# Residual adds between blocks, copies of the first unit's fourth slab, and VectorE in written order

## The chip, the cores and the metric

The kernel runs on one core of one Trainium2 chip. The metric is the time of one execution on the device in microseconds (us); lower is better. The core has a matrix engine (TensorE, PE in the profile), three engines for elementwise work (VectorE or DVE, ScalarE or ACT, GpSimd or POOL) and SyncE (SP), whose queue issues nearly all DMA transfers here. Each engine takes its own instructions in a fixed order and waits for the others by semaphores. TensorE writes its results to PSUM, in banks of 128 x 512 float32 values; tiles that are kept longer lie in SBUF.

## The reference

Eight sequences `x[b]` of 512 rows and 256 columns go through nine gated experts (eight with a gate per sequence and expert, and a shared one), and the input is added at the end. All is float32.

```python
g = jnp.einsum('bsd,edf->ebsf', h, Wg)
u = jnp.einsum('bsd,edf->ebsf', h, Wu)
expert_outs = jnp.einsum('ebsf,efd->ebsd', jax.nn.silu(g) * u, Wd)
expert_output = jnp.einsum('be,ebsd->bsd', gating_probs, expert_outs)
shared = jnp.einsum('bsf,fd->bsd', jax.nn.silu(h @ Sg) * (h @ Su), Sd)
return (1.0 - sg) * expert_output + sg * shared
# and then: x = x + that
```

The hidden size F is 1024.

## The kernel before

**Tiling.** The eight sequences form two halves (`h` = 0, 1) of four. Within a half, each expert's hidden columns are cut into two groups (`g`) of four slabs of 128 columns. A half, an expert and a group make a *unit*: 2 x 9 x 2 = 36 units, one after the other. A unit multiplies four sequences by four slabs. It does so with fewer products than the plain way: sums and differences of the operands are formed, for the four points `CI` = 0, 1, -1, 2 and the six pairs of `PAIRS`, and the results are put together from them.

**A unit on TensorE.** `hub_steps` lists the steps on the four diagonal combinations: `P_step` (L458) starts a bank, `Q_step` (L481) adds to it. From the bank's state after P, ScalarE keeps a copy `P` (L464, slabs 0 to 2), and VectorE forms differences `f` between slabs (L474, L476); for slab 3 they read the bank itself and overwrite the copies. After Q, ScalarE makes `sg` = silu(bank) (L444) or VectorE makes `h` = sg x gate x bank (L449), for the gate half (m = 0) and the up half (m = 1); ScalarE keeps `D`, a copy of the bank (L488, L491). Then come the six pairs. For each pair, `seed` fills a bank from `f` (L498, ScalarE), `R1_step` adds a product of `v` (a difference of inputs) and `u` (one of weights) to it (L503), and at once makes the bank of the other direction, `D` minus this one (L508, VectorE). `R_step` adds the products of `b` and `wb` to both banks (L513); for the second direction VectorE adds `D` (L518). Their `h` go to `h_sums`, which makes `X`, the difference of the pair's two `h` (L529), and notes the sums of `h` that GpSimd adds later (L540, `rows` and `cols`).

**The down product** of a unit (`down`) runs interleaved with the second half of the same unit and the first half of the next one. `pair` makes three steps for each pair: `r` (L595), then `S` or `s` (L579, L595), then the product with `X` on top of `r` (L618). Its results are collected in accumulators in SBUF: `accB`, `accV` and `accb`, by VectorE (L566 to L570). For pairs 0 to 3 `S` is carried on: ScalarE copies `accS` into a PSUM bank (L578), TensorE adds to it, ScalarE copies it back (L587); `b` likewise. Two PSUM banks (`po0`, `po1`) serve all of this in turn. In the last `down` of each half (`closes`) the accumulators are combined (L622).

**The order.** The strings `ORDER`, `FIRST` and `LAST` write out how gate/up steps (G), down steps (D), input turns (T) and the last unit's products (X) alternate: a unit is `HUB` (GGD eight times) and six times `BLOCK` (GGDGGDGGD). The engines in `HAND` (L843: PE and Pool; for the first unit ScalarE too, L846) take their instructions as written. VectorE's and the other engines' instructions are placed by a scheduler. `AHEAD_AT` and `BACK_AT` name the D steps at which `prepare` (the second half's inputs) and `turn_back` do a piece.

**First unit.** Its inputs are turned on TensorE; `v` and `b` are computed by VectorE and GpSimd (`x_difference`, `x_sums`) and stored to DRAM, from where all later units load them (L292, L309). `v` tiles share three buffers, `b` two, `wb` two.

**Ends of the halves.** Results are kept transposed, in 32 x 32 squares. For the first half, `turn_back` (L663) reloads the sequence from DRAM into a tile of `iopool` (two buffers; L659), transposes a result on VectorE (L669), adds it (L670) and issues four stores (L673). These pieces run in the second half's first unit. For the last unit, `end_step` turns what is there so far, stores it to DRAM as rows and loads it back (`endin`, L707), loads the input rows (L150), lets GpSimd add both (L711), and `store_rows` adds the last products (L729) and stores.

Of the kernel before, what the change touches and what calls it, by code (L numbers as in the profile page):

```python
# [16 lines left out]
def kernel(  # L17
# [104 lines left out]
    back = {}  # L122
# [18 lines left out]
    def load_rows(pool, tag, b):  # L141
        rows = []
        for c in range(2):
            if pool is not xpool:
                t = pool.tile([P, 2, D], F32, tag=tag, name=f"xin{b}_{c}")
            elif c == 0:
                both = pool.tile([P, NT, D], F32, tag=tag, name=f"xin{b}")
            if pool is xpool:
                t = both[:, 2 * c : 2 * c + 2]
            nc.sync.dma_start(  # L150
                t, x[b].rearrange("(p t) d -> p t d", t=NT)[:, 2 * c : 2 * c + 2, :]
            )
            rows.append(t)
        return rows


    def squares(a, b, q):

        return a[b].rearrange("s (k q d) -> q s k d", k=2, d=32)[q]
# [122 lines left out]
    def x_difference(u, p):  # L282

        i, j = PAIRS[p]
        v = vpool.tile([P, S], F32, tag="v", name=f"v{u.name}_{p}")
# [169 lines left out]
    def P_step(u, i, m):  # L455
# [6 lines left out]
        if i < 3:  # L462
            t = ppool.tile([P, S], F32, tag="p", name=f"P{i}{m}_{u.name}")
            nc.scalar.copy(t, bank)  # L464
            u.Ps[i, m] = t
        for p, (k, j) in enumerate(PAIRS):
# [33 lines left out]
    def R1_step(u, p, m):  # L500
# [5 lines left out]
        other = new_bank(u, m, f"c{i}{j}")  # L506
        u.bank[i, j, m] = other
        ve.tensor_sub(other, u.Ds[j, m], bank)  # L508
# [142 lines left out]

    BACK = [(0, 1), (0, 0), (2, 1), (2, 0), (1, 1), (1, 0), (3, 1), (3, 0)]

    def load_back(h, i):

        if (h, i) not in back:
            xr = iopool.tile([P, S // 32, 2, 32], F32, tag="io", name=f"xr{h}_{i}")
            for q in range(4):
                nc.sync.dma_start(xr[ts(q, 32)], squares(x, NI * h + i, q))  # L659
            back[h, i] = xr  # L660
        return back[h, i]

    def turn_back(h, i, r):  # L663

        b = NI * h + i
        block = ends.pop((h, i, r))
        xr = load_back(h, i)
        t = zpool.tile([P, S], F32, tag="z", name=f"to{b}_{r}")
        ve.transpose(t, block)  # L669
        ve.tensor_add(xr[:, :, r], t.rearrange("p (c d) -> p c d", d=32), xr[:, :, r])  # L670
        if (i, 1 - r) not in BACK[BACK.index((i, r)):]:
            for q in range(4):
                nc.sync.dma_start(squares(out, b, q), xr[ts(q, 32)])  # L673
            if i in (0, 2):
                load_back(h, i + 1)
# [5 lines left out]
    end_stores = []  # L681

    def end_step(kind, i):

        b = NI * (NH - 1) + i
# [5 lines left out]
        elif kind == "store":  # L691
            to = end_rows[i] = dram.tile([S, D], F32, tag=f"end{i}", name=f"endrows{i}")
            at = to.rearrange("(c r t) d -> r t c d", r=32, t=NT)
            for r in range(2):
                for q in range(4):
                    end_stores.append((
# [3 lines left out]
        elif kind == "x":  # L700
            last_rows[i] = load_rows(xpool, "x", b)
        elif kind == "load":
            at = end_rows[i].rearrange("(p t) d -> p t d", t=NT)
            end_rows[i] = []
            for c in range(2):
                t = sumpool.tile([P, 2, D], F32, tag="sum", name=f"endin{i}_{c}")
                nc.sync.dma_start(t, at[:, 2 * c : 2 * c + 2])  # L707
                end_rows[i].append(t)
        else:
            for xr, t in zip(last_rows[i], end_rows[i]):  # L710
                gp.tensor_tensor(xr, xr, t, ALU.add)  # L711
# [13 lines left out]
    def store_rows(j, c):  # L725
        b = NI * (NH - 1) + j
        xr = last_rows[j][c]
# [12 lines left out]
    def gate_up(u, nxt):  # L740
# [18 lines left out]
        step = 0  # L759
        for kind, i, m in hub_steps(u):  # L760
# [6 lines left out]
            elif kind == "P":  # L767
                P_step(u, i, m)
                if u.n == 0 and m == 1 and i in (1, 3):
                    for p, make in ahead[:2] if i == 1 else ahead[2:]:  # L770
                        make(u, p)
            else:
                R1_step(u, 0, m)
            step += 1
# [5 lines left out]
        if u.n == 0:  # L780
            make_ad(u)
            for p in range(len(PAIRS)):
                d_forms(u, p)
        for p in range(len(PAIRS)):
# [13 lines left out]
            for m in range(2):  # L798
                if not last:
                    R1_step(u, p + 1, m)  # L800
                    if m == 0 and u.n == 0 and p and p + 1 < len(PAIRS):
                        sums(p + 1)
# [3 lines left out]
                for r in range(2):  # L806
                    R_step(u, p, m, r)
                    if m == 1 and r == 1:
# [3 lines left out]
                        if p + 2 < len(PAIRS) and u.n:  # L812
                            sums(p + 2)
# [15 lines left out]
        7: (("turn", 0), ("store", 0)), 16: (("turn", 1), ("store", 1)), 18: (("x", 0),),  # L829
        20: (("turn", 2), ("store", 2), ("x", 1)), 22: (("load", 0), ("x", 2)),  # L830
        24: (("turn", 3), ("store", 3), ("x", 3)), 28: (("add", 0),), 30: (("load", 1),),
        34: (("add", 1),), 37: (("load", 2),), 40: (("add", 2),), 44: (("load", 3),),
        47: (("add", 3),),
# [7 lines left out]
    AHEAD_AT = (8, 11, 14, 17, 20)  # L841
    BACK_AT = (6,10,11,13,15,18,20,23)
    HAND = {mybir.EngineType.PE, mybir.EngineType.Pool}  # L843
    by_hand = ExitStack()
    by_hand.enter_context(
        tc.manual_schedule(engines=HAND | {mybir.EngineType.Activation})  # L846
# [18 lines left out]
    for u in units:  # L865
# [6 lines left out]
        for what in FIRST if u.n == 0 else LAST if nxt is None else ORDER:  # L872
            if what == "G":
                if nG == TAKE:
                    for _ in behind:
                        pass
                    if u.opens:
                        acc = {}
                    behind = down(u, acc) if nxt is not None else iter(())
                if final and nxt is not None and nG in (18, 21, 24, 27):  # L880
                    load_x(u.h + 1, (nG - 18) // 3)
                if final and nxt is not None and nG in (30, 36):
                    load_back(u.h, (nG - 30) // 3)
                if nxt is None:
                    for what_, i in END_STEPS.get(nG, ()):
                        end_step(what_, i)
                    if end_stores:
# [71 lines left out]
```

## Time and profile before

Three runs took 2445.75, 2446.47 and 2447.15 us. One execution was profiled.

| what | value |
|---|---|
| median of the runs | 2446.47 us |
| the profiled execution, its own time | 2446.47 us |
| its span, first to last instruction | 2444.7 us |
| TensorE clock granted, mean | 0.999 |
| wait of a `b` load for landing, median from issue | 3.6 us |
| one `X` (L529), mean | 982 ns |
| one `h` (L449), mean | 743 ns |

The page gives, for each engine, the time in which it was busy and the number of its instructions. A group of instructions is named by its source line, engine and operation, and `out<-in` by the program's tile names with their numbers left out. A float32 matmul of 128 x 512 appears as two passes. A timeline row holds the start from the beginning of the span, the duration, the engine, the line, the operation and, in brackets, how long the engine had been idle before it and what released it. A wait row holds the waiting engine and its line, what it waited for, the total in us, how often, and the longest.

### The profile page before, as it was taken

How to read it: one execution, taken by the hardware profiler on the slowest of the kernel's cores; microseconds unless marked ns; L12 is line 12 of the kernel's file. 1: busy time of each engine (PE TensorE's matmuls, PEld its weight loads, DVE VectorE, ACT ScalarE, POOL GpSimd, SP SyncE). 2: the span in 40 equal slices, each digit the busy share in tenths (PEclk: the TensorE clock that was granted, in tenths of full speed). 3: DMA queues.
4: the chain of work that ended last, by engine and by line, in shares of the span. 5: the costliest groups of instructions: out<-in, count | busy, mean ns of one | idle time of the engine just before them, and what ended most of it. 6: DMA issues, size and time to landing. Idle time of an engine off the chain costs nothing.

```text
span 2444.7 us, 22778 instructions
## 1 busy us (share of the span) xinstructions
PE 2431.5 (99%) x5736; PEld 1085.1 (44%) x5736; DVE 1928.9 (79%) x2870; ACT 1239.4 (51%) x2294; POOL 2080.0 (85%) x2313
## 2 busy tenths in 40 slices
PE   9999999999999999999999999999999999999999
PEld 4444444444444444444444444444444444444446
DVE  7778878777777877787987777777777777777795
ACT  5555554554555555555445555555555555555542
POOL 8988888898988989898878888888888888888872
PEclk9999999999999999999999999999999999999999
DMA  4333343343433333344353233323333333233245
GB/s 158 101 105 111 104 112 112 103 134 102 126 110 97 105 111 97 106 129 125 112 118 120 85 95 91 91 81 99 99 104 103 95 97 92 88 91 92 86 117 149
DMA packets 237841, 260.02 MB, mean 106 GB/s; under 512 B 80656, under 2 KB 173072, under 8 KB 237712
## 3 DMA queue, kind: packets, MB, share of 16 engines
q1 hardware_dynamic: 236880, 258.27, 35.9%
q8 instruction: 48, 0.79, 0.1%
q14 instruction: 81, 0.66, 0.1%
q10 hardware_dynamic: 832, 0.30, 0.0%
HBM read 240.69 MB, written 17.83 MB: 106 GB/s over the span
## 4 chain that ended last, share of the span: by engine, by line
PE 96%; POOL 1%; DVE 1%; DMA 1%; issue 0%; ACT 0%; SPq 0%; ACTq 0%; DVEq 0%; POOLq 0%
PE c L513 30%; PE c L503 15%; PE c L481 10%; PE c L458 10%; PE r L595 7%; PE r L618 7%; PE S L579 5%; PE b L579 5%; PE q L595 5%; PE s L595 2%; PE tail L720 1%; DMA sgt<-ondB_sharedgateprob_dram 0%; POOL wd L429 0%; POOL wb L396 0%; DVE h L449 0%
## 5 line engine op out<-in xcount | busy, mean ns | idle before, releaser
L513 PE MATMUL c<-b,wb 128*128 128x512 f32 x1728 | 848.1, 593 | 2.6 <-DMA b<-xs 1.9
L444 ACT ACTIVATE sg<-c 128x512 f32<-128x512 f32 x576 | 343.8, 597 | 595.0 <-DVE c L518 343.7
L449 DVE SCALAR_TENSOR_TENSOR h<-sg,coef,c 128x512 f32<-128x512 f32 x576 | 427.8, 743 | 235.6 <-PE c L513 128.3
L513 PEld LDWEIGHTS c<-b,wb 128*128 128x128 f32 x1728 | 328.3, 190 | 412.9 <-issue 390.0
L503 PE MATMUL c<-v,u 128*128 128x512 f32 x864 | 441.5, 593 | 1.9 <-ACT c L498 1.4
L540 POOL TENSOR_TENSOR rows<-rows,h 128x512 f32<-128x512 f32 x280 | 369.0, 1318 | 0.0
L508 DVE TENSOR_TENSOR c<-D,c 128x512 f32<-128x512 f32 x432 | 298.7, 692 | 81.1 <-ACT sg L444 61.4
L540 POOL TENSOR_TENSOR cols<-cols,h 128x512 f32<-128x512 f32 x280 | 357.7, 1277 | 0.0
L518 DVE TENSOR_TENSOR c<-c,D 128x512 f32<-128x512 f32 x432 | 298.6, 691 | 22.3 <-PE c L513 22.1
L396 POOL TENSOR_TENSOR wb<-u,wb 128x256 f32<-128x256 f32 x108 | 79.2, 733 | 237.3 <-ACT wb L394 237.3
L458 PE MATMUL c<-x,w 128*128 128x512 f32 x572 | 274.5, 592 | 0.0
L503 PEld LDWEIGHTS c<-v,u 128*128 128x128 f32 x864 | 163.0, 189 | 210.0 <-issue 163.9
L595 PE MATMUL r<-h,wd 128*128 128x512 f32 x420 | 215.4, 594 | 0.0
L618 PE MATMUL r<-X,ud 128*128 128x512 f32 x420 | 214.5, 592 | 0.0
L529 DVE TENSOR_TENSOR X<-h,h 128x512 f32<-128x512 f32 x210 | 206.1, 982 | 6.8
L481 PE MATMUL c<-x,at 128*128 128x512 f32 x432 | 209.4, 593 | 1.2 <-DVE P L474 0.7
L491 ACT COPY D<-c 128x512 f32<-128x512 f32 x284 | 165.8, 584 | 83.8 <-DVE h L449 83.8
L540 POOL TENSOR_TENSOR rows<-h,h 128x512 f32<-128x512 f32 x140 | 195.4, 1396 | 0.0
L540 POOL TENSOR_TENSOR cols<-h,h 128x512 f32<-128x512 f32 x140 | 181.0, 1293 | 0.0
L464 ACT COPY P<-c 128x512 f32<-128x512 f32 x216 | 126.6, 587 | 106.9 <-PE c L458 102.3
L458 PEld LDWEIGHTS c<-x,w 128*128 128x128 f32 x572 | 108.5, 190 | 135.9 <-issue 111.9
L578 ACT COPY S<-accS 128x512 f32<-128x512 f32 x132 | 77.9, 590 | 149.8 <-DVE accV L566 140.7
(108 smaller groups left out, 3472.5 us busy)
## 6 DMA issues: line engine op xcount, KB each, us to landing
b<-xs SPq DMA_DIRECT2D x210, 512.0 KB, 3.6
v<-xs SPq DMA_DIRECT2D x210, 256.0 KB, 2.6
wd<-in_L_cond_Wd_dram SPq DMA_DIRECT2D x32, 512.0 KB, 4.9
w<-in_L_cond_Wg_dram SPq DMA_DIRECT2D x127, 128.0 KB, 3.5
w<-in_L_cond_Wu_dram SPq DMA_DIRECT2D x127, 128.0 KB, 3.6
f<-xd SPq DMA_DIRECT2D x12, 512.0 KB, 3.6
xs<-f SPq DMA_DIRECT2D x18, 256.0 KB, 3.0
xin<-in_x_dram SPq DMA_DIRECT2D x16, 256.0 KB, 4.1
```

Of the source, the lines that this page charges most:

```text
L444: nc.scalar.activation(s, bank, AF.Silu)
L449: ve.scalar_tensor_tensor(t, u.sg[i, j], coef[:, u.e, b : b + 1], bank, ALU.mult, ALU.mult)
L458: nc.tensor.matmul(bank, u.raw[i][:, m, 0], xhub[u.h, i][:, 0], start=True, stop=True)
L481: nc.tensor.matmul(bank, u.at[i][:, m], xhub[u.h, i][:, 1], start=False, stop=True, skip_group_check=True,)
L503: nc.tensor.matmul(bank, u.U[p][:, m], u.V[p], start=False, stop=True, skip_group_check=True)
L508: ve.tensor_sub(other, u.Ds[j, m], bank)
L513: nc.tensor.matmul(bank, u.W[p][:, r, m], u.VB[p][:, r], start=False, stop=True, skip_group_check=True,)
L518: ve.tensor_add(bank, bank, u.Ds[j, m])
L540: gp.tensor_tensor(sums[n], u.h_[n, n] if first else sums[n], u.h_[at], ALU.add)
L579: nc.tensor.matmul(po, w, b, start=not full, stop=True, skip_group_check=full)
L595: nc.tensor.matmul(po, w, b, start=True, stop=True)
L618: nc.tensor.matmul(A, u.Ud[p], u.X[p], start=False, stop=True, skip_group_check=True)
```

## The change

Five things change.

- VectorE joins the engines whose instructions stand as written, in the whole program. The making of the other direction's bank (L508) becomes a function of its own, `other_step`, which is called one or two steps later than `R1_step`.
- The first unit's slab 3: ScalarE copies both banks after P into tiles of `sumpool`, and the six differences read the copies. The `v` and `b` of the first unit are made at other steps, two `v` lie in `iopool` tiles, and GpSimd's `b`, `wb` of a pair stand ahead of sums.
- The residual is no longer added at the ends. `residual` adds the inputs, which lie in SBUF all the time, to the accumulators: 14 VectorE operations in each half, three in each of its units 11 to 15 (14 in all), at the D steps 13, 18 and 23.
- `turn_back` transposes straight into the tile that is stored; the reload of the input and the add go away. Its stores are put in a list, from which one is issued at each G step.
- At the end, the loads of the input rows and GpSimd's adds go away; one load of 512 KB instead of two brings the turned rows back.

TensorE has the same instructions in the same order. VectorE has 20 more, GpSimd 8 fewer.

```diff
-        v = vpool.tile([P, S], F32, tag="v", name=f"v{u.name}_{p}")
+        if u.n == 0 and p in (3, 4):
+            v = iopool.tile([P, 2, S], F32, tag="io", name=f"v{u.name}_{p}")[:, 0]
+        else:
+            v = vpool.tile([P, S], F32, tag="v", name=f"v{u.name}_{p}")
...
-        if i < 3:
-            t = ppool.tile([P, S], F32, tag="p", name=f"P{i}{m}_{u.name}")
+        if i < 3 or u.n == 0:
+            pool, tag = (ppool, "p") if i < 3 else (sumpool, "sum")
+            t = pool.tile([P, S], F32, tag=tag, name=f"P{i}{m}_{u.name}")
             nc.scalar.copy(t, bank)
             u.Ps[i, m] = t
+            if i == 3:
+                bank = t
...
-        other = new_bank(u, m, f"c{i}{j}")
-        u.bank[i, j, m] = other
-        ve.tensor_sub(other, u.Ds[j, m], bank)
+
+    def other_step(u, p, m):
+        i, j = PAIRS[p]
+        other = u.bank[i, j, m] = new_bank(u, m, f"c{i}{j}")
+        ve.tensor_sub(other, u.Ds[j, m], u.bank[j, i, m])
...
+    def residual(acc, h):
+        for i in range(NI):
+            c, b, B = CI[i], acc["b", i], acc["B", i]
+            v, A = xhub[h, i][:, 0], xhub[h, i][:, 1]
+            for to, x_, s in ((b, v, 1.0), (b, A, c), (B, A, 1.0 + c * c), (B, v, c)):
+                if s == 1.0:
+                    ve.tensor_add(to, to, x_)
+                elif s == -1.0:
+                    ve.tensor_sub(to, to, x_)
+                elif s != 0.0:
+                    ve.scalar_tensor_tensor(to, x_, s, to, ALU.mult, ALU.add)
+                else:
+                    continue
+                yield
...
     def turn_back(h, i, r):
-        xr = load_back(h, i)
-        t = zpool.tile([P, S], F32, tag="z", name=f"to{b}_{r}")
-        ve.transpose(t, block)
-        ve.tensor_add(xr[:, :, r], t.rearrange("p (c d) -> p c d", d=32), xr[:, :, r])
+        t = backs[i]
+        ve.transpose(t[:, :, r], ends.pop((h, i, r)).rearrange("p (c d) -> p c d", d=32))
         if (i, 1 - r) not in BACK[BACK.index((i, r)):]:
             for q in range(4):
-                nc.sync.dma_start(squares(out, b, q), xr[ts(q, 32)])
-            if i in (0, 2):
-                load_back(h, i + 1)
+                outgoing.append((at[q], t[ts(q, 32)]))
...
-        elif kind == "x":
-            last_rows[i] = load_rows(xpool, "x", b)
-        elif kind == "load":
+        else:
             at = end_rows[i].rearrange("(p t) d -> p t d", t=NT)
-                nc.sync.dma_start(t, at[:, 2 * c : 2 * c + 2])
+            last_rows[i] = xpool.tile([P, NT, D], F32, tag="x", name=f"endin{i}")
+            nc.sync.dma_start(last_rows[i], at)
-        else:
-            for xr, t in zip(last_rows[i], end_rows[i]):
-                gp.tensor_tensor(xr, xr, t, ALU.add)
...
             else:
                 R1_step(u, 0, m)
+                other_step(u, 0, m)
+            if u.n == 0 and (kind, i, m) in first:
+                p, make = ahead[first.index((kind, i, m))]
+                make(u, p)
...
                 for r in range(2):
                     R_step(u, p, m, r)
+                    if r == 0 and not last:
+                        other_step(u, p + 1, m)
                     if m == 1 and r == 1:
                         h_sums(u, p)
...
-                        if p + 2 < len(PAIRS) and u.n:
+                        if p + 2 < len(PAIRS):
                             sums(p + 2)
...
+    REST_IN, REST_AT = range(11, 16), (13, 18, 23)
-    HAND = {mybir.EngineType.PE, mybir.EngineType.Pool}
+    HAND = {mybir.EngineType.PE, mybir.EngineType.Pool, mybir.EngineType.DVE}
...
-                    if end_stores:
-                        nc.sync.dma_start(*end_stores.pop(0))
+                if outgoing:
+                    nc.sync.dma_start(*outgoing.pop(0))
...
+                if nD in REST_AT and u.n % (len(units) // NH) in REST_IN:
+                    next(rest, None)
```

## The prediction

> **What bounds the kernel now.** I read the page first, then all waits of TensorE, then one steady unit and three special stages as timelines, engine by engine.
>
> ```profile
> span 2444.7 us, 22778 instructions
> PE 2431.5 (99%) x5736; PEld 1085.1 (44%) x5736; DVE 1928.9 (79%) x2870; ACT 1239.4 (51%) x2294; POOL 2080.0 (85%) x2313
> PE 96%; POOL 1%; DVE 1%; DMA 1%; issue 0%; ACT 0%; SPq 0%; ACTq 0%; DVEq 0%; POOLq 0%
> ```
>
> TensorE works through the whole span and the chain that ended last is its own. A unit takes 66.95 us again and again: 78 matmuls of two passes, 0.858 us each. Nothing can be won inside a steady unit; any wait that is put in is paid 30-odd times. What TensorE waits for is all in one short list (line, releaser: total, times, longest):
>
> ```profile
> PE S L579 <- ACT S L578: 2.3, 4, 0.6
> PE c L513 <- DMA b<-xs: 1.9, 1, 1.9
> PE c L503 <- ACT c L498: 1.4, 1, 1.4
> ```
>
> The order of TensorE's instructions is the same before and after, instruction for instruction. So I only ask how much earlier or later the others release it.
>
> **1. The carried sums in a steady unit (the main term).** The `S` matmul (L579) adds to a PSUM bank that ScalarE first fills from `accS` (L578), and that bank is free only when VectorE has added the previous pair's result to `accV` (L566). Before, the scheduler put `accV` ahead of the second `h` (L449) and of `X` (L529). In written order (`h_sums` runs inside the gate step, the `accV` step after it) it stands behind both. One such place, VectorE, then ScalarE, GpSimd and TensorE:
>
> ```profile
> 645.80 0.69 DVE L518 TENSOR_TENSOR c<-c,D 128x512 f32<-128x512 f32 x1
> 646.40 0.68 DVE L566 TENSOR_TENSOR accV<-r,accV 128x512 f32<-128x512 f32 x1
> 647.00 0.74 DVE L449 SCALAR_TENSOR_TENSOR h<-sg,coef,c 128x512 f32<-128x512 f32 x1
> 647.77 1.23 DVE L529 TENSOR_TENSOR X<-h,h 128x512 f32<-128x512 f32 x1
> ```
> ```profile
> 647.12 0.59 ACT L578 COPY S<-accS 128x512 f32<-128x512 f32 x1 [1.14 <-DVE accV L566]
> ```
> ```profile
> 647.18 1.28 POOL L540 TENSOR_TENSOR rows<-h,h 128x512 f32<-128x512 f32 x1
> 648.41 1.19 POOL L384 TENSOR_TENSOR u<-at,at 128x256 f32<-128x256 f32 x1
> ```
> ```profile
> 650.17 1.02 PE L579 MATMUL S<-h,wd 128*128 128x512 f32 x2
> ```
>
> The reader should see that `X` started at 647.77 but ended at 649.00, 0.59 after GpSimd's `rows` gave way to `u` at 648.41: both operands of `X` lie in SBUF, and it sat out GpSimd's instruction. Now the new order. An `h` that stands directly behind the `c+D` it reads starts 0.82 later:
>
> ```profile
> 638.01 0.69 DVE L518 TENSOR_TENSOR c<-c,D 128x512 f32<-128x512 f32 x1
> 638.83 0.75 DVE L449 SCALAR_TENSOR_TENSOR h<-sg,coef,c 128x512 f32<-128x512 f32 x1
> ```
>
> So `h` starts at 645.80 + 0.82 = 646.62, `X` 0.77 later at 647.39. That is 0.21 after `rows` began, so `X` still ends at 649.00. `accV` starts 0.08 before that end, ends at 649.60; the copy runs 649.63 to 650.22. From the end of such a copy the first pass needs another 0.155: 0.05 to the weight load and 0.10 for the load that nothing hides. This comes from a place where TensorE does wait (copy 1185.85 + 0.59 = 1186.44, weights at 1186.49, two passes 0.96 apart from the next matmul instead of 0.858):
>
> ```profile
> 1185.85 0.59 ACT L578 COPY S<-accS 128x512 f32<-128x512 f32 x1 [1.80 <-DVE accb L568]
> 1186.49 1.13 PE L579 MATMUL S<-h,wd 128*128 128x512 f32 x2 [0.56 <-ACT S L578]
> ```
>
> 650.22 + 0.155 = 650.38 against 650.17: TensorE loses about 0.2. The same sum for all 93 such places of the 31 steady units gives 62 with a loss (`S1` and `S3`, 0.23 mean) and 31 without, most with about 0.33 to spare (`S2`, where `X` gets through sooner). VectorE's step before it and GpSimd's `rows` are both released by TensorE, so the loss comes back in each unit: 62 x 0.23 = **+14.4 us**. Bounds: 0 if `X` gets in ahead of `rows`; +21 if `S2` loses 0.2 as well.
>
> **2. The two closing units.** There VectorE is busy 29.88 of 30 us, and the copy for `S` waits for the last of L622 and two additions to `b`. L622 moves behind `X`, whose end GpSimd fixes. So two of the three copies come 0.60 later, one 0.34 later, and the matmul `s` 0.60 later. All four already wait, so all is paid: 2 x 2.14 = **+4.3 us** (0 to +6).
>
> **3. The first unit.** Gain: two `v` and two `b` no longer stand ahead of the four `f` subtractions, so the `Q` matmuls of slab 2 do not wait (-0.9), and those of slab 3 wait for two copies instead of six subtractions (-1.0). TensorE would stand at R1 of pair 1 at 25.2. Loss: the six subtractions of the fourth slab wait for ScalarE's two new copies, behind two seed copies (to 23.0), then six at 0.60 end at 27.0 instead of 26.1. The second `v`, before at 14.1, now follows at 27.7, so the R1 matmul of pair 1 goes at 27.9 instead of 27.1. Queued behind: GpSimd's half of that pair's `b` needs this `v`, and everything on GpSimd follows. It ended at 24.6 before, at 29.0 now. Carried through GpSimd's list, the first half of `wb` for pair 2 is ready at 44.9 instead of 39.97, and its R matmul goes at 45.0 instead of 41.27 (+3.7). Back comes VectorE's wait
>
> ```profile
> 39.32 1.20 DVE L288 TENSOR_TENSOR v<-x,x 128x512 f32<-128x512 f32 x1 [2.61 <-POOL b L303]
> ```
>
> and with it TensorE's 1.4 us at L503. Later `wb` are listed ahead of sums, which wins back 1.8 on GpSimd: the last `wb` comes at 70.2, not 67.19. I take **+3.0** (from -5, all waits of the first 70 us gone, to +5, with a clock loss below).
>
> **4. Opening of the second half.** SP has four x loads and eight stores ahead of pair 3's `b`. Without the loads, and with the stores let out one per gate step, six stores remain ahead of it (the last two wait for a turn that ends near 1250), so it is issued near 1252 rather than 1258.5; the copies into the row tiles also leave VectorE earlier. What the wait cost:
>
> ```profile
> 1262.98 1.79 PE L513 MATMUL c<-b,wb 128*128 128x512 f32 x2 [1.91 <-DMA b<-xs]
> 1264.56 1.91 PE L595 MATMUL r<-h,wd 128*128 128x512 f32 x2
> ```
>
> Passes here are 0.85 apart, not 0.43; the granted clock was 0.5 for 3.41 us. Row: 2.07 + 1.76 = 3.8. [...] I go by the row. With four smaller waits there (0.41, 0.05, 0.70, 0.29) the gain is **-5.3** (by the rule -3.5).
>
> **5. What hides.** The 28 residual adds (three per unit in ten units) stand ahead of steps where VectorE idles 1.3 to 1.8 us per pair. Nearest row: `X`, 0.69 alone, up to 1.6. [...] Neither reaches TensorE while the idle time of its stage is longer: 0, and up to +2 if one in ten misses. The turns for the last block wait for row-tile stores, with 2 us to spare; the eight GpSimd additions and loads that go there were hidden: 0. The end (last pass to last store, 3.8 us) stays.
>
> **Sum:** 14.4 + 4.3 + 3.0 - 5.3 = +16.4 on the profiled execution's own 2446.47 us (span 2444.7 and 1.8 around it), which is the median of the runs: **2462.9 us**.
>
> **Rivals.**
> *`X` wins SBUF (not slower).* Place: `X` against `rows` in each S1 and S3. If `X` starts 0.22 earlier, it ends at 647.9, `accV` at 648.5, and no copy is late. Term 1 goes: 2448.5, no change. For: only 0.2 decides. Against: in this trace `X` and `b` that started 0.06 to 0.3 behind a GpSimd instruction always sat it out. Chance 0.12.
> *VectorE released early.* The first unit loses its waits (-5), the opening gains 5.3, no seed is late: 2446.5 - 10 + 4 = 2440. For: before, VectorE stood 2.6 us for GpSimd. Against: the arithmetic of steps 1 and 3. Chance 0.06.
> *More is late.* `S2` joins, residual adds push seeds, the first unit pays its clock: 14.4 + 7 + 6 + 2 + 5 - 5.3, 2475. For: VectorE can no longer step around a waiting instruction. Against: 0.3 to spare at S2. Chance 0.17.
> Forecast: 0.65.
>
> **Numbers.** Low 2449 includes the edge of the first rival, high 2471 half of the third. A difference of 0.2% (4.9 us) is about what a measurement of this kernel can tell from none. Slower: 0.65 + 0.17 + 0.02 = 0.84; same 0.10; faster 0.06.
>
> **What would show it.** A new long row `S L579 <- ACT S L578` with some 60 short waits; `accV` behind `X`; a unit's period near 67.4 instead of 66.95; no wait for `b<-xs` near 1260. Wrong if the period stays 66.95, if `X` starts ahead of `rows`, or if waits sit in the ten residual units alone.

## The result, and the profile after

The changed kernel takes 2472.7 us (median of 4 runs, 2471.6 to 2473.43) against 2446.4 (2445.75 to 2447.15). The ratio is 1.0107 with a 95% interval of 1.0095 to 1.0119: slower by 26.3 us where +16.4 had been forecast. The direction and the largest term were right. The size was not: 2472.7 lies above the stated high of 2471. The profiled execution is the slowest of the four (2473.43), so the account by stage below is of 26.96 us, not 26.3.

The page of the changed kernel, with span, instructions, busy time by engine and the chain that ended last:

```profile
span 2471.4 us, 22597 instructions
PE 2446.8 (99%) x5736; PEld 1080.6 (44%) x5736; DVE 2004.4 (81%) x2890; ACT 1239.6 (50%) x2296; POOL 2070.4 (84%) x2305
PE 94%; DVE 3%; POOL 1%; ACT 1%; issue 0%; DMA 0%; DVEq 0%; SPq 0%; POOLq 0%; ACTq 0%
```

TensorE runs the same 5736 matmuls and is as "busy" as before (99%), yet the span is 26.7 us longer. VectorE has 20 instructions more and 75 us more of busy time, and its share of the chain went from 1% to 3%. The list of TensorE's waits has new rows (line, releaser: total, times, longest):

```profile
PE S L579 <- ACT S L578: 6.6, 6, 1.3
PE c L500 <- DVE v L282: 3.3, 1, 3.3
PE c L500 <- ACT c L495: 2.4, 2, 1.4
PE c L500 <- POOL u L378: 2.0, 1, 2.0
PE c L500 <- POOL cols L540: 1.8, 1, 1.8
PE s L595 <- DVE accb L570: 1.2, 2, 0.6
PE c L513 <- DMA b<-xs: 0.7, 1, 0.7
```

Two warnings for the reader. The 60 short waits before `S` in the steady units, the largest loss of all, are not in this list: each is 0.13 us, under what it lists (0.15), and behind it the second pass comes 0.10 late (in the place shown below its weight load starts at 185.86, 0.11 behind the first pass; in the kernel before, at an `S` on time, both start at 650.17). And the releasers `u` and `cols` are not the true ones, as the experiments show. So I took the loss from the starts of the matmuls instead: a matmul of 512 columns follows the one before by 0.429 us when nothing is late, and what is beyond that (gaps of more than 0.04 us) was summed by stage. The last two columns are runs of the next section.

| Stage (us lost by TensorE) | before | changed | forecast change | measured change | changed, VectorE scheduled | before, only the order |
|---|---|---|---|---|---|---|
| start and first unit | 6.9 | 10.6 | +3.0 | +3.7 | 9.7 | 6.7 |
| steady units, both halves | 0 | 16.3 | +14.4 | +16.3 | 3.8 | 15.2 |
| two closing units | 4.3 | 9.9 | +4.3 | +5.6 | 4.3 | 9.9 |
| opening of the second half | 5.6 | 2.8 | -5.3 | -2.8 | 0.3 | 4.6 |
| last unit | 0.3 | 4.4 | 0 | +4.0 | 0.3 | 4.9 |
| sum | 17.1 | 43.9 | +16.4 | +26.8 | 18.4 | 41.3 |

With VectorE scheduled, the steady units lost 3.8 us in five places; these were not taken apart. The sum, +26.8, agrees with the profiled executions (2473.43 - 2446.47 = +26.96), so nothing is lost outside TensorE's gaps.

**The steady place**, in the changed kernel: timelines of VectorE, ScalarE, GpSimd and TensorE (start, duration, instruction, idle time before it).

```profile
181.28 0.69 DVE L518 TENSOR_TENSOR c<-c,D 128x512 f32<-128x512 f32 x1
182.10 0.75 DVE L443 SCALAR_TENSOR_TENSOR h<-sg,coef,c 128x512 f32<-128x512 f32 x1
182.89 1.59 DVE L529 TENSOR_TENSOR X<-h,h 128x512 f32<-128x512 f32 x1
184.40 0.68 DVE L566 TENSOR_TENSOR accV<-r,accV 128x512 f32<-128x512 f32 x1
```
```profile
185.11 0.59 ACT L578 COPY S<-accS 128x512 f32<-128x512 f32 x1 [1.11 <-DVE accV L566]
```
```profile
182.65 1.27 POOL L540 TENSOR_TENSOR rows<-h,h 128x512 f32<-128x512 f32 x1
183.88 1.18 POOL L378 TENSOR_TENSOR u<-at,at 128x256 f32<-128x256 f32 x1
```
```profile
184.77 1.02 PE L500 MATMUL c<-v,u 128*128 128x512 f32 x2
185.75 1.12 PE L579 MATMUL S<-h,wd 128*128 128x512 f32 x2
```

`h` follows `c+D` by 0.82, `X` starts 0.24 behind `rows` and ends 0.60 after `rows` gives way, `accV` follows, and the copy for `S` ends at 185.70. `S` could have started at 184.77 + 0.858 = 185.63; it starts at 185.75, and its second pass is 0.10 late too.

**The last unit**, VectorE and TensorE. This was not foreseen:

```profile
2414.80 0.69 DVE L508 TENSOR_TENSOR c<-D,c 128x512 f32<-128x512 f32 x1
2418.59 0.71 DVE L693 STREAM_TRANSPOSE end<-accb 128x512 f32<-128x512 f32 x1 [3.11 <-DMA endrows<-end]
2419.22 0.67 DVE L693 STREAM_TRANSPOSE end<-accB 128x512 f32<-128x512 f32 x1
2419.82 0.67 DVE L518 TENSOR_TENSOR c<-c,D 128x512 f32<-128x512 f32 x1
2420.39 0.73 DVE L443 SCALAR_TENSOR_TENSOR h<-sg,coef,c 128x512 f32<-128x512 f32 x1
```
```profile
2421.83 1.88 PE L500 MATMUL c<-v,u 128*128 128x512 f32 x2 [2.02 <-POOL u L378]
```

The turn of the fourth block (L693) waits 3.11 us for a buffer that the second block's stores still read. In written order everything behind it waits too: `c+D`, `h`, the next seed, and R1 on TensorE. In the kernel before, the same turn ran here, with no idle time ahead of it:

```profile
2401.07 0.70 DVE L689 STREAM_TRANSPOSE end<-accb 128x512 f32<-128x512 f32 x1
```

There the scheduler had put seven instructions ahead of it that stand behind it in written order. In the changed kernel the clock follows the wait: for 3.41 us TensorE is granted half of it, so that passes start 0.85 us apart instead of 0.43 (a half clock, from here on). Busy time by engine in two stretches, with the granted clock (PEclk) before DMA's share and GB/s:

```profile
2414.00:2421.00 7.00, 5.81 (x20) 3.26 (x18) 3.89 (x7) 2.12 (x5) 1.41 (x3) 1.00 0.82 204
2421.50:2426.00 4.50, 4.17 (x8) 2.06 (x9) 1.70 (x3) 1.37 (x3) 0.18 (x1) 0.62 1.07 274
```

**The opening.** The wait for `b` is gone; instead R1 is 2.0 us late near 1274 us. VectorE and ScalarE there:

```profile
1271.29 0.66 DVE L518 TENSOR_TENSOR c<-c,D 128x512 f32<-128x512 f32 x1
1273.28 0.75 DVE L443 SCALAR_TENSOR_TENSOR h<-sg,coef,c 128x512 f32<-128x512 f32 x1 [1.33 <-POOL rows L540]
```
```profile
1272.36 0.58 ACT L562 COPY accS<-S 128x512 f32<-128x512 f32 x1 [1.99 <-PE S L579]
1274.93 0.58 ACT L562 COPY accV<-r 128x512 f32<-128x512 f32 x1 [1.99 <-PE r L618]
1275.41 0.60 ACT L438 ACTIVATE sg<-c 128x512 f32<-128x512 f32 x1
1276.05 0.59 ACT L495 COPY c<-P 128x512 f32<-128x512 f32 x1
```

One reading is the row with `rows`: `h` waits for a buffer that GpSimd frees late. Another is ScalarE: `sg` could have run when `c+D` ended at 1271.95, but it stands behind two copies that wait for TensorE, and the seed of R1 behind it. An experiment below decides between them.

### The profile page after: what moved, and what is told of

It reads as the page before. It is cut to its first block, busy times and chain, and to the rows that moved or that the text cites. A ratio compares the mean times of both kernels' runs of the same rounds, so it can differ in the third digit from the quotient of the medians.

```text
span 2471.4 us, 22597 instructions
## 1 busy us (share of the span) xinstructions
PE 2446.8 (99%) x5736; PEld 1080.6 (44%) x5736; DVE 2004.4 (81%) x2890; ACT 1239.6 (50%) x2296; POOL 2070.4 (84%) x2305
## 4 chain that ended last, share of the span: by engine, by line
PE 94%; DVE 3%; POOL 1%; ACT 1%; issue 0%; DMA 0%; DVEq 0%; SPq 0%; POOLq 0%; ACTq 0%
PE c L513 28%; PE c L500 14%; PE c L452 10%; PE c L478 10%; PE r L595 7%; PE r L618 7%; PE S L579 5%; PE q L595 5%; PE b L579 5%; PE s L595 2%; PE tail L716 1%; DVE h L443 1%; DVE X L529 0%; DVE P L471 0%; DVE accb L570 0%
## 5 line engine op out<-in xcount | busy, mean ns | idle before, releaser
L508 DVE TENSOR_TENSOR c<-D,c 128x512 f32<-128x512 f32 x432 | 298.0, 691 | 83.6 <-ACT sg L438 63.9
L529 DVE TENSOR_TENSOR X<-h,h 128x512 f32<-128x512 f32 x210 | 249.0, 1186 | 7.2
L618 PE MATMUL r<-X,ud 128*128 128x512 f32 x420 | 214.6, 592 | 0.7 <-ACT accB L562 0.7
L495 ACT COPY c<-P 128x512 f32<-128x512 f32 x216 | 128.3, 594 | 135.3 <-DVE h L443 131.3
```

Of the source, the lines that this page charges most:

```text
L508: ve.tensor_sub(other, u.Ds[j, m], u.bank[j, i, m])
L529: ve.tensor_sub(u.X[p], u.h_[j, i], u.h_[i, j])
L618: nc.tensor.matmul(A, u.Ud[p], u.X[p], start=False, stop=True, skip_group_check=True)
```

## Experiments

Every kernel ran on the same chip as runs of the kernel before; times are medians. The first question is which part of the change costs: the order, or the work that it moves.

**The order undone, all else kept.**

```diff
-    HAND = {mybir.EngineType.PE, mybir.EngineType.Pool, mybir.EngineType.DVE}
+    HAND = {mybir.EngineType.PE, mybir.EngineType.Pool}
...
-        tc.manual_schedule(engines=HAND | {mybir.EngineType.Activation, mybir.EngineType.DVE})
+        tc.manual_schedule(engines=HAND | {mybir.EngineType.Activation})
```

> The changed kernel with VectorE's order left to the scheduler again; residual adds, copies, loads and stores stay as changed. Theory (the loss is VectorE's written order): most of the 26 us come back, 2449 (2444 to 2454), with waits before S under 3 us in all. Rival (the moved residual adds and the copies cost time by themselves): 2460 or more.

2447.58 us; ratio 1.0004 (0.9996 to 1.0013). No wait before `S` is left in the steady units, the last unit's wait is gone, and the opening lost 0.3 us instead of 5.6: the 5.3 us that had been forecast there. The first unit kept its loss (8.7 us against 5.2 before, without the start).

**The order alone, in the kernel before** (from its second unit on, with `other_step` called later as in the change).

```diff
...
                     R_step(u, p, m, r)
+                    if r == 0 and not last:
+                        other_step(u, p + 1, m)
...
-            by_hand.enter_context(tc.manual_schedule(engines=HAND))
+            by_hand.enter_context(tc.manual_schedule(engines=HAND | {mybir.EngineType.DVE}))
```

> The kernel before with VectorE in written order from the second unit on, and with the difference c moved behind the first R step as in the change (the order written before would not run without it); residual work, first unit and ends as before. Theory: +14 for S in the steady units and +4 to +6 in the two closing units, so 2466 (2461 to 2470), with waits of about 0.23 us before S twice a unit. Rival (the order costs only together with the residual adds and the new stores): under 2453.

2470.64 us; ratio 1.0098 (1.0082 to 1.0113), just above the expected 2461 to 2470: the last unit, which was not in that sum, lost 4.9 us here too. By the two runs the written order costs 24.5 us in the kernel before (2470.64 - 2446.15) and 25.1 in the changed one (2472.7 - 2447.58), and all the rest of the change together 1.4 to 2.1.

**`X` behind the down-projection step**, so that `accV` is ahead of it (from the second unit on).

```diff
                     if m == 1 and r == 1:
-                        h_sums(u, p)
+                        if u.n:
+                            late.append((u, p))
+                        else:
+                            h_sums(u, p)
...
             if what == "G":
+                flush_late()
...
                 next(behind, None)
+                flush_late()
```

> From the second unit on, X is written behind the next down-projection step, so that accV's add comes before it on VectorE; nothing else moves. Theory (the steady loss is accV standing behind X in VectorE's written order, so that ScalarE's copy for S starts late): the 14.1 us of waits before S in the steady units fall to under 1, and some of the 8.2 us in the two closing units go as well, so 2472.7 falls by 14 to 20, to about 2455. Rival A (S is late because VectorE has no room, whatever the order): the waits stay within 3 us of where they are, or come back before R1. Rival B (X is itself needed early): X's own readers, the third matmuls of a pair, become late and show new waits before L618.

2459.69 us, 13.0 down, where 14 to 20 had been expected. VectorE and ScalarE at the place shown above:

```profile
182.09 0.75 DVE L443 SCALAR_TENSOR_TENSOR h<-sg,coef,c 128x512 f32<-128x512 f32 x1
182.75 0.68 DVE L566 TENSOR_TENSOR accV<-r,accV 128x512 f32<-128x512 f32 x1
183.35 1.10 DVE L529 TENSOR_TENSOR X<-h,h 128x512 f32<-128x512 f32 x1
```
```profile
183.88 0.59 ACT L578 COPY S<-accS 128x512 f32<-128x512 f32 x1
```

The copy starts 1.2 us earlier and waits for nothing. In the steady units all 14.1 us before `S` went to 0, and each closing unit went from 5.0 to 2.8. The time fell by less than that since about 6 us came up elsewhere: R1 was 0.5 to 0.8 us late in eight of the ten units that have residual adds. In the changed kernel only one unit of each half showed it, with 0.5.

**The sums one step later**, `X` and `accV` as changed.

```diff
-                if nG > TAKE and nG % 2 == 0 and u.sums:
+                if nG > TAKE and nG % 2 == 1 and u.sums:
```

> The changed kernel with GpSimd's row and column sums written one step later (odd steps of the blocks instead of even ones). If the steady loss needs X to start behind a GpSimd sum (X takes 1.59 us then, 0.7 to 1.0 us otherwise) and the later sum leaves X alone, the 0.23 us waits before S at S1 and S3 go: 2458 (2454 to 2462). If the sums still meet X one step on, or if accV would be late behind an X of 0.8 us as well: 2470 to 2475.

2466.93 us, between the two times that had been expected. Both cases are in one unit; VectorE, then GpSimd:

```profile
190.22 1.72 DVE L529 TENSOR_TENSOR X<-h,h 128x512 f32<-128x512 f32 x1
...
198.29 1.06 DVE L529 TENSOR_TENSOR X<-h,h 128x512 f32<-128x512 f32 x1
```
```profile
190.11 1.27 POOL L540 TENSOR_TENSOR rows<-h,h 128x512 f32<-128x512 f32 x1
...
198.76 1.72 POOL L540 TENSOR_TENSOR cols<-cols,h 128x512 f32<-128x512 f32 x1
```

The first `X` starts 0.11 behind `rows` and takes 1.72; its `S` is 0.25 late. The second starts 0.47 ahead of its sum and takes 1.06, and its `S` is on time. Over the kernel, the late places moved with the sums. In the changed kernel 29 were at the `S` of pair 1, 29 at that of pair 3 and two at that of pair 2 (`S1`, `S3`, `S2`); here 28 of 34 are at `S2` and three each at the others. The number of `X` that start less than 0.3 us behind a sum went the same way: 28, 25 and none of 35 for pairs 1, 3 and 2, then one, one and 26. So the steady loss needs both: `accV` behind `X`, and `X` behind a GpSimd sum. A late place costs more than before (0.33 on the mean, against 0.235).

**The last turn six steps later.**

```diff
-        20: (("turn", 2), ("store", 2)), 24: (("turn", 3), ("store", 3)),
+        20: (("turn", 2), ("store", 2)), 30: (("turn", 3), ("store", 3)),
```

> The last unit's turn of its fourth block and the stores behind it move from step 24 to step 30; nothing else. Theory (the transposes wait 3.1 us for a buffer that the second block's stores still read, and everything behind them on VectorE waits too): the 2.19 us wait before R1 near 2419 us and the half clock behind it, 3.96 us in all in the last unit, fall to under 0.7, so 2469 (-3 to -4). Rival (the wait belongs to GpSimd's u, which the list of waits names): the wait stays, and the time stays at 2472 to 2473.

2469.21 us, 3.5 down. VectorE's turn there:

```profile
2424.26 0.70 DVE L693 STREAM_TRANSPOSE end<-accb 128x512 f32<-128x512 f32 x1
2424.89 0.67 DVE L693 STREAM_TRANSPOSE end<-accB 128x512 f32<-128x512 f32 x1
```

It waits for nothing; the 4.0 us are gone, and the row that blamed `u` is gone from the list of waits.

**Are the residual adds hidden?** Both runs have `X` behind the step and the last turn late; one has no residual adds (its output lacks the input), the other gives them out elsewhere.

```diff
-                if nD in REST_AT and u.n % (len(units) // NH) in REST_IN:
+                if nD in REST_AT and u.n % (len(units) // NH) in ():
```
```diff
-    REST_IN, REST_AT = range(11, 16), (13, 18, 23)
+    REST_IN, REST_AT = range(11, 16), (13, 16, 19)
```

> X behind the step and the last turn late, as in the run of the three edits together but with v where the change put it, and without the residual adds (x is left out of the output). Theory (in the five units with residual adds of each half, one of them stands ahead of the sum before h and makes R1 late by about 0.8 us, ten times): against 2456 with the adds, 2448 (2446 to 2451). Rival (VectorE is full there anyway, the sums are late with or without): 2454 to 2457.

> X behind the step and the last turn late, residual adds kept but given out at down-projection steps 13, 16 and 19 of a unit instead of 13, 18 and 23, so that each follows a step whose sum ScalarE carries, and none follows a VectorE add. Theory (only the add at step 18 collides, with accB's): as without the adds, 2448 to 2450. Rival (any add of 1 to 1.7 us in a block is too much): 2454 or more.

2451.27 us and 2450.83 us: no difference that these runs can tell, both slightly above what was expected, and no late R1 in the residual units of either. With the adds where the change has them it was 2458.36 (the run of three edits further down, whose third edit by itself gained nothing). The adds collide where they follow a VectorE add of the same step. From the run with `X` behind the step, VectorE at such a place:

```profile
796.15 0.68 DVE L566 TENSOR_TENSOR accB<-r,accB 128x512 f32<-128x512 f32 x1
796.86 1.68 DVE L659 TENSOR_TENSOR accB<-accB,x 128x512 f32<-128x512 f32 x1
798.46 0.69 DVE L518 TENSOR_TENSOR c<-c,D 128x512 f32<-128x512 f32 x1
```

Behind an `accB`, 1.68 us of residual add (step 18) push `c+D`, `sg` and the seed. At steps 13, 16 and 19 ScalarE carries the sum, and VectorE has a hole.

**The first unit.** Two edits were tried alone in the changed kernel:

```diff
-    first = [("P", 1, 1), ("Q", 2, 1), ("P", 3, 1)]
+    first = [("P", 1, 1), ("Q", 1, 1), ("Q", 2, 1)]
```

> In the first unit alone, the second pair's difference v is written before the third slab's subtractions, ahead of the last three of the fourth slab, and the first pair's b earlier as well. Theory (the second pair's R1 waits at 24.4 us for v, which stands behind the six subtractions): the 3.46 us wait falls below 1, the half clock behind it (4 passes, 1.7 us) goes, and a part of it comes back at the next pairs: 2469 (-2 to -5). Rival (GpSimd's b half and weight forms bound the first unit): the wait goes but the next ones grow by as much, 2471 to 2473.

2472.63 us: nothing, as the rival had it. The wait moved from R1 (3.46 us) to the next R (4.9 us), which now waits for the `c` difference behind the same six subtractions.

```diff
-        if i < 3 or u.n == 0:
+        if i < 3:
```

> The changed kernel without ScalarE's copies of the first unit's fourth slab: the six subtractions read the banks again. Theory (a subtraction that reads only SBUF shares its access with GpSimd: the six take 5.09 us here and took 3.67 us from the banks before): v comes 1.4 us earlier, the 3.46 us wait at 24.4 us falls to about 2, and the half clock behind it may go: 2470 (2468.5 to 2471.5). Rival (the copies free the banks earlier and so pay): the next waits for a bank grow, 2473 or more.

2472.09 us, above the expected range: the wait for `v` went, and a wait of 2.7 us with a half clock came at the following pair's R1. The three edits together (`X`, turn, `v`):

> The three edits together: X behind the step, the last turn late, v earlier. Theory (three separate waits that add up): -14 to -20, -3 to -4 and -2 to -5, so about 2448 (2444 to 2454), level with the kernel before within 0.2 per cent or ahead of it. Rival (they share their cover, VectorE is full): the sum falls short by more than 5 us, 2456 or more.

2458.36 us, 14.3 down and not the 19 to 29 expected; alone, the three took 13.0, 3.5 and 0.1. On top of the residual adds' new places, with `v` early, four of the six subtractions were kept until the first block was done:

```diff
+                if u.n == 0 and p > 3:
+                    kept.append(ops)
...
+                        while kept:
+                            ve.tensor_sub(*kept.pop(0))
```

> The written order with X behind the step, the last turn late and the residual adds at steps 13, 16 and 19, and in the first unit v earlier and four of the fourth slab's six subtractions (the last two pairs') kept until the first block is done. Theory (in the first unit whatever stands behind the six subtractions in VectorE's order is late: v in the changed kernel, the difference c when v goes ahead): the wait of 3 to 5 us near 25 us falls below 1 and the half clock behind it goes: against 2450.8 without these two edits 2446 (2444 to 2448.5). Rival (GpSimd's b half bounds the first unit): no gain, 2450 to 2452.

2453.94 us, worse than the 2450.83 without: the four then ran in one piece of 5.14 us and R1 of a later pair waited 5.2. No other place for them was tried. Two more runs left VectorE to the scheduler, put the first unit back as before, and kept the better residual places, without the copies and with them.

```diff
             if u.n == 0 and m == 1 and i in (1, 3):
                 for p, make in ahead[:2] if i == 1 else ahead[2:]:
                     make(u, p)
...
                     if m == 0 and u.n == 0 and p and p + 1 < len(PAIRS):
                         sums(p + 1)
```

> VectorE left to the scheduler, residual adds at steps 13, 16 and 19, first unit as before (no copies, v and b made where they were), and the rest as changed: lighter opening, the last block's rows. Theory (the parts that pay without the written order are kept, 5.3 us at the opening; those that cost are gone, 3.5 us in the first unit and 2 to 3 us of residual adds): 2441.5 (2439.5 to 2444), ahead of the kernel before by 0.1 to 0.3 per cent. Rival (what is saved at the opening comes back elsewhere): 2445 to 2448.

> The run with VectorE under the scheduler and the first unit as before, with ScalarE's copies of the first unit's fourth slab put back and nothing else. If the copies are what costs in the first unit (SBUF subtractions of up to 1.75 us against 0.68): waits of 7 us or more there, 2447 (2446 to 2449). If the places of v and b are: waits near 5 us and 2444 to 2445.

2444.53 us without the copies, just outside the expected 2439.5 to 2444, and 2447.92 with them, as expected. The six subtractions on VectorE, without and with:

```profile
22.03 3.67 DVE L468 TENSOR_TENSOR P<-P,c 128x512 f32<-128x512 f32 x6
```
```profile
22.74 6.81 DVE L468 TENSOR_TENSOR P<-P,P 128x512 f32<-128x512 f32 x6 [0.78 <-ACT P L456]
```

The copies turn a subtraction with one operand in PSUM into one with both in SBUF. Its twin on GpSimd (`b`, two of them) goes from 2.50 to 3.39 us in the same two runs. So with the copies the six took 3.14 us longer on VectorE and the two 0.89 us longer on GpSimd. The copies cost 4.2 us of TensorE's time in the first unit (5.05 against 9.25, half clock included), and 3.4 us of the medians. The copies are thus enough for that loss by themselves, but with the written order and the new places of `v` and `b` it stays even without them (8.8). Which of these two does that was not tried apart.

**The opening's 2.0 us.** ScalarE was put by hand in that stretch, and the seeds written one block earlier.

```diff
-            if not last and u.n:
+            if not last and (u.n not in (0, 18) or u.n and p == 0):
                 seed(u, p + 1)
...
-                        if u.n == 0 and p + 2 < len(PAIRS):
+                        if u.n in (0, 18) and p + 2 < len(PAIRS):
                             seed(u, p + 2)
...
+                    if u.n == 18:
+                        by_hand.close()
+                        by_hand.enter_context(
+                            tc.manual_schedule(engines=HAND | {mybir.EngineType.Activation})
+                        )
...
-        if u.n == 0:
+        if u.n in (0, 18):
             by_hand.close()
             by_hand.enter_context(tc.manual_schedule(engines=HAND))
```

> The changed kernel with ScalarE by hand in the second part of the opening unit (from the first block's end), and with that unit's seeds written one block earlier, ahead of the step whose accV copy waits for TensorE; VectorE's order and all else stay. Theory (the 2.0 us wait before R1 near 1274 us comes from ScalarE's order: sg and the seed stand behind copies that wait for TensorE): that wait goes, the opening loses 0.8 us or less instead of 2.8, 2470.7 (2470 to 2472). Rival (the wait is VectorE's h, whose buffers GpSimd's sums free late because X sits behind them): it stays at 2.0, 2472 to 2473.5.

2470.07 us. ScalarE, at the place shown above:

```profile
1272.28 0.60 ACT L438 ACTIVATE sg<-c 128x512 f32<-128x512 f32 x1 [1.49 <-DVE c L518]
1272.77 0.58 ACT L562 COPY accS<-S 128x512 f32<-128x512 f32 x1
1273.24 0.61 ACT L495 COPY c<-P 128x512 f32<-128x512 f32 x1
```

`sg` and the seed are ahead of the copies, and R1 follows L618 with no wait. The opening lost 1.6 us, of which 0.9 is new and sits at the end of that unit, where the edit hands ScalarE back to the scheduler. So the wait was ScalarE's order (the hand order and the earlier seeds were not tried apart). The row with `rows` was no more than the event nearest in time: the `h` that it blames starts 1.13 us behind the start of TensorE's passes at 1272.15, and in this run the same `h` starts 1.13 behind them too (1272.83 and 1271.70). ScalarE was left to the scheduler in the changed kernel as before; that it was ordered so came with VectorE's written order: R1 was 2.0 late here with the order alone as well, and on time with VectorE scheduled. Of the 2.6 us of time only about 1 is from the opening: the last unit's wait came without its half clock in this run (2.0 us lost instead of 4.0).

**Can both be had?** One run keeps the written order from the second unit on, with the first unit as before under the scheduler; the other has it in the steady units alone (its edit is shown).

```diff
-        if u.n == 0:
+        if u.n in (0, 16, 18, 33):
             by_hand.close()
-            by_hand.enter_context(tc.manual_schedule(engines=HAND))
+            more = {mybir.EngineType.DVE} if u.n in (0, 18) else set()
+            by_hand.enter_context(tc.manual_schedule(engines=HAND | more))
```

> Written order from the second unit on, with X behind the step, the last turn late and the residual adds at steps 13, 16 and 19; the first unit as before and under the scheduler. Theory (the first unit's loss is in its own parts): against 2450.8 the first unit gives back 4 to 5 us, 2446 (2444.5 to 2447.5), the waits at the opening stay at 2.75 us and those of each closing unit at 2.8. Rival (a late first unit was absorbed later): 2449 or more.

> As the run with the first unit alone under the scheduler, but the first, both closing, the opening and the last unit are left to the scheduler, and only the steady units between them have VectorE in written order. Theory: steady waits as in the written order (0.9 and 0), opening 0.3 and closings 2.1 each as under the scheduler, first unit 5: about 11.5 us of waits in all, 2441.5 (2440 to 2443.5), ahead of the kernel before. Rival (the change of order at the borders costs what it saves): 2444 or more.

2447.02 us, as expected, and 2444.36 us, above the expected 2440 to 2443.5: the mix loses 1.3 us at the opening instead of 0.3, with the same new 0.9 at the end of that unit. The first unit went to 5.8 and 5.1. The mix has the least waits of all (12.8 us, against 17.1 before); its ratio is 0.9992 (0.9984 to 1.0001), that of the scheduled one without copies 0.9996 (0.9987 to 1.0004). Both lie 1.3 to 1.9 us below the kernel before in the median and cannot be told from it by these runs.

## Why the prediction was right or wrong

- **Step 1, steady units: right.** Forecast 62 places of 0.23 at `S1` and `S3`, +14.4 (62 x 0.23 is 14.3); measured 58 places there and two at `S2`, 0.235 on the mean, 14.1. Shown by three runs: order alone, `X` behind the step, sums one step later. A unit takes 67.4 us, as written. That a row of some 60 short waits would show them was wrong: the list of waits leaves them out.
- **Step 2, closing units: right in kind, 1.3 too small.** Per closing unit +2.8 instead of +2.14. The mis-sized term is the copy at `S2`, put at 0.34 later: TensorE lost 0.7 more there, and 0.7 at each of the other three places instead of 0.60.
- **Step 3, first unit: near in size (+3.7 for +3.0), in part by luck.** The gains came (1.9 us of waits before the `Q` matmuls fell to 0.1). R1 of the second pair went at 28.27 (27.9 forecast), by two errors that nearly cancel: the six subtractions, put at 0.60 each, took 5.09 us instead of 3.67, since the copies had put their second operand into SBUF, but they began about 1 us earlier than forecast. The `wb` of the third pair was ready at 44.88 as forecast (44.9), and its R went at 45.04 (45.0). Yet it did not wait for `wb`: TensorE had by then lost 6.5 us by itself, 3.46 in the wait for `v`, 1.7 in the half clock behind it (four passes, left to the upper end of the range) and 1.2 before a seed. The 1.4 us before L503 did come back, but 0.8 and 1.6 came before L618 and the next pair's R1 (51.88 and 54.42), which no term had.
- **Step 4, opening: the step failed by half.** The load of `b` was issued earlier as forecast, the wait for it and its half clock went, and with VectorE scheduled the full 5.3 came (0.3 us left of 5.6). In the changed kernel 2.8 are left: 2.1 since ScalarE's `sg` and seed were ordered behind copies that wait for TensorE, and 0.7 in two short waits that were not taken apart. The 3.5 that the step sets beside its 5.3 is the same sum without the 1.76 us of half clock; no run shows a rule by which this wait would have been free of it. I had followed the loads and stores, and did not look at the order of the other engines in that stage.
- **Step 5, "the turns for the last block wait for row-tile stores, with 2 us to spare ... 0": this failed most, +4.0 for 0.** The turn takes one of two buffers, and the stores that free it go out one a step, so the last of the eight leaves about when the turn is reached: the buffer came 3.1 us late. In the kernel before, the scheduler had placed the turn behind other work, so it did not wait; what was not asked is what would be queued behind it in written order. Of the 4.0, the wait of R1 is 2.2 and the half clock behind it 1.7, which did not come in five other runs with waits of 1.96 to 2.54 us there (last section). Moving the turn by six steps took the 4.0 us away.
- **Step 5, residual adds: 0 forecast, 1.0 measured** (R1 0.48 us late in one unit of each half), and about 6 once `S` no longer held TensorE back. The test "shorter than the idle time of its stage" is one of sums; what counts is the one slot, with the instruction ahead of it and the one that waits behind it.
- **The rest of the steady units**, about 1 us, is for the most part one R at 663.19, which waited for its load of `b` (the row `b<-xs` of the list). Why that load landed late was not taken apart.
- **Rivals.** "`X` wins SBUF" decided by 0.2 us as told: `X` starts 0.24 behind `rows`. "More is late" (2475) came nearest in time, and its reason, that VectorE can no longer step around a waiting instruction, is what the turn showed. Its terms were others: `S2` held but for two places, the residual adds gave 1.0 of its 6, the first unit's clock 1.7 of its 5, and the last unit's turn was not in it.

Taken together: of the 10.4 us missed, 4.0 are the last turn, 2.5 the opening, 1.9 the steady units' other waits, 1.3 the closing units and 0.7 the first.

## What to carry to other kernels

Before an engine's order is written by hand, list every instruction in it that waits for something outside its own stage (a buffer that stores read, another engine's sum), and look at what stands behind each: the scheduler had let other work pass them. The written order took 25 of the 26 us, of which 14 stand at `accV` behind `X` and 4 behind the last turn. Look at the order of the engines that are still scheduled as well: it changes with it. Where an instruction takes longer beside another engine's (`X` took 1.59 us behind `rows` at 182.89, 0.69 alone), put the one that others wait for ahead of it (`accV` ahead of `X`). A wait of 0.1 us at 60 places is found in the distances of the bottleneck's starts, not in a list of waits.

## What the runs showed of the hardware

- In these runs a half clock did not go by the length of the wait alone. In the last unit R1 lost 2.19 us in the changed kernel, and a half clock followed (0.50 from 2422.02 to 2425.43 us); at the same matmul 2.54 us in the run with `X` behind the step, and 1.96 to 2.04 in four other runs, were followed by none. Stretches of 3.41 us around this wait, in the changed kernel and with `X` behind the step (busy time of PE, PEld, DVE, ACT and POOL, then the granted clock):

```profile
2418.61:2422.02 3.41, 1.39 (x6) 0.79 (x5) 3.38 (x6) 1.91 (x4) 2.09 (x3) 1.00 0.67 173
2422.02:2425.43 3.41, 3.41 (x5) 1.35 (x5) 1.18 (x2) 0.59 (x1) 0.00 (x0) 0.50 1.10 269
```
```profile
2405.64:2409.05 3.41, 2.55 (x8) 1.14 (x6) 1.73 (x3) 0.73 (x2) 1.08 (x2) 1.00 0.83 145
2409.05:2412.47 3.42, 1.90 (x5) 0.98 (x6) 2.85 (x5) 1.56 (x3) 1.01 (x2) 1.00 1.06 290
2412.47:2415.88 3.41, 3.41 (x14) 2.25 (x13) 1.40 (x2) 1.58 (x4) 0.00 (x0) 1.00 0.69 177
```

  The 2.19 us lie in the first stretch of the changed kernel. Of the 2.54 us 1.03 lie in the first and 1.51 in the second of the other run, and the clock stayed at 1.00 in all three. What made the difference is not shown. In the 3.41 us ahead of the other two half clocks of the kernel before and the changed one (the ends of the span aside) TensorE was busy for 1.44 us (kernel before, 1259.83 to 1263.24, then 0.50 for 3.41 us) and 0.99 us (changed kernel, 25.86 to 29.27, then the same). So a wait of about 2 us at this matmul cost 1.7 us more in the changed kernel and nothing more in five other runs.
- GpSimd took longer as well: with the copies in place, three small differences (128x128) of the first unit took 0.90 us each beside the six SBUF subtractions on VectorE, and 0.45 in the run without the copies.
